# Moving the first experts' weight loads and the normalised-token stores from SP's to ScalarE's transfer queue

## The chip, the cores and the metric

The kernel runs on one core of a Trainium2 chip. The metric is the device time of one execution in microseconds (us); where several executions were timed, their median is given. The names used for the engines are: PE for TensorE (matrix products), DVE for VectorE, ACT for ScalarE, POOL for GpSimd, and SP for SyncE, which in this kernel issues nearly all plain transfers. "Queue" means the line of transfers that one engine issues: SP's, ACT's or POOL's.

## What is computed

The kernel takes 4 × 1024 tokens of width 256, lets them attend to 77 context rows with 16 heads, adds the result, and then runs a mixture of nine experts on the normalised tokens, two experts per token. Cut to what matters:

```python
q = layernorm(x) @ Wq                      # and a scale and shift per head
k, v = split(layernorm(ctx) @ Wkv)
x = x + softmax(q k^T / 8) v @ Wout
xn = (x - mean) / sqrt(var + 1e-5)         # "normalised tokens"
w, idx = top_k(softmax(xn @ Wr), 2)        # two experts per token
hidden = silu(xn @ Wg[e]) * (xn @ Wu[e])   # 256 -> 704
out = x + sum over the two e of w_e * (hidden @ Wd[e])
```

All of it is float32.

## The kernel before

**Two stages.** The tokens are cut into 8 groups (`NG`) of 512, each into 4 sub-blocks (`NS`) of 128. The loop at L1667 runs over the 32 sub-blocks (`i`), with a thirty-third turn that only drains. After it, the loop at L1792 runs over the expert blocks: each takes up to 256 tokens of one expert, gathered through an index list.

**One turn of the attention loop.** PE makes the scores of sub-block `i` in three PSUM banks (`scores`, L295). DVE takes the maxima (L307), ACT the 16 exponentials (`exponentials`, L318), DVE scales them into `an` (L340, L345) and turns them in blocks of 32 (L356) into `anT`. `weights_turn` (L352) sends `anT` to a buffer in device memory, `a_d` (L357); `weights_back` (L360) reads it back in another order with four transfers into `aT` (L366). Both go out from SP. PE uses `aT` of sub-block `i - 3` in `values` (L372), so a sub-block has about three turns for the way out and back. `anT` exists once, so DVE may not turn the next sub-block until `a_d` has landed; `aT` exists three times.

**Once per group.** Counted from the group's last sub-block, the turns are told apart by `sr`. In the turn with `sr == 1` the residual `x` goes to the output (L945) and ACT takes a root. In the turn with `sr == 2` ACT makes the normalised tokens `y` of the group with four activations (`normalised`, L977 to L985). The store of `y` to `y_d` (L988) is put into the list `written` and issued in the same turn after `weights_back` (L1756); for the last two groups it is issued at once (L990). For group 6 that is in the thirty-third turn, for group 7 within the first expert blocks. `y` exists once.

**Weights of an expert block.** `load` (L1360) reads the expert's number from a table into a register (`values_load`), and issues six transfers: the gate weights `Wg` (704 KB), three pieces of the up weights `Wu` (64, 128 and 512 KB) and two of the down weights `Wd` (640 and 64 KB). It is a generator with a stop after `Wg`, after `Wu` and after `Wd`. For the first two blocks (`LEAD = 2`), `first_fetch` (L1658) calls `weights(j, True)`; their generators land in `partly`. The loop takes one step of them per turn (L1752): block 0's `Wg`, `Wu`, `Wd` go out in turns 27, 28 and 29, the one step more that is left ends the generator in turn 30, and all of block 1's go out after the loop (L1766). From block 2 on, `fetch` (L1597) issues a block's weights whole.

**Order of the work.** The order on each engine is that in which the code lists it; nothing is moved by a scheduler. Each engine takes its own list in order, so an instruction that waits holds up those behind it on its engine. The engine that issues a transfer waits for whatever the transfer needs, then goes on once it has issued it.

**The first expert block** (`hidden_pair`, L1437) begins while the last two sub-blocks' `values` are still to be done: after the block's first sixth comes `values(30)`, after the fourth `values(31)` (L1788). For each sixth PE fills one of five PSUM tiles (`mm_tile`), ACT applies Silu (L1450) and DVE multiplies (L1451), which frees the tile. `values` takes a tile of the same five.

Of the kernel before, what the change touches and what calls it, by code (L numbers as in the profile page):

```python
# [15 lines left out]
P = 128  # L16
# [5 lines left out]
def kernel(  # L22
# [18 lines left out]
    nc = tc.nc  # L41
# [6 lines left out]
    E, _, FF = wg.shape  # L48
# [4 lines left out]
    NS = TB // P  # L53
    NG = TOK // TB
    GPB = N // TB
    NF = FF // P
    FT = FF - NF * P
# [55 lines left out]
    y_d = dram.tile([TOK, D], F32, name="y_d")  # L113
# [143 lines left out]
    def off_mean(name, g, mv, r):  # L257

        o = stat.tile([P, NS], F32, tag=name, name=f"{name}{g}")
        nc.vector.scalar_tensor_tensor(o, mv[:, :, 0], -1.0, r, ALU.mult, ALU.mult)  # L260
        return o
# [136 lines left out]
    with ExitStack() as kvs:  # L398
# [23 lines left out]
        for i in range(2):  # L422
            at = slice(i * BH, (i + 1) * BH)
            nc.sync.dma_start(out=cx[:J, at], in_=ctx_in[at].rearrange("b j d -> j b d"))
        wk_v = wkv[:, :INNER].rearrange("(c p) n -> p c n", p=P)
        for i in range(2):
            at = slice(i * INNER // 2, (i + 1) * INNER // 2)
# [226 lines left out]
        def router_weights(pm):  # L654
# [20 lines left out]
            out=before, in_=ones, pattern=[[1, P]], compare_op=ALU.is_gt, fill=0.0, base=0,  # L675
# [48 lines left out]
        for n in range(NP):  # L724
# [7 lines left out]
            for c in range(C):  # L732
                for t in range(2):
# [8 lines left out]
                    at = slice(h * J, (h + 1) * J)  # L742
# [165 lines left out]
    for b in range(B):  # L908
        for m in range(2):
            at = 2 * b + m  # L910
# [66 lines left out]
    def normalised(g):  # L977

        y = pools["rpool"].tile([P, NS, D], F32, tag="y", name=f"y{g}", bufs=1)
        r = routed[g]["r"]  # L980
        o = off_mean("fo", g, routed[g]["mv"], r)
        for s in range(NS):
            yield nc.scalar.activation(
                y[:, s, :], xg[g][:, s, :], AF.Identity,
                bias=o[:, s : s + 1], scale=r[:, s : s + 1],  # L985
            )
        written.append(
            lambda: nc.sync.dma_start(out=y_d.rearrange("(g p s) d -> g p s d", p=P, s=NS)[g], in_=y)  # L988
        )
        if g > NG - 3:  # L990
            written.pop()()
# [108 lines left out]
    tabs = {}  # L1100
# [154 lines left out]
    FA = 4 * P  # L1255
    FB = FF - FA
# [34 lines left out]
    def of(tiles, j):  # L1291

        return tiles[j % len(tiles)]
# [30 lines left out]
    def weights(j, in_parts=False):  # L1324

        _, i, kind = blocks[j]
        if kind == "quad2":
            wgus[j], downs[j] = quads.pop(i)
            return
        if j == LAST:  # L1330
            w, d = late["w", uppers[j][0]], late["d", uppers[j][0]]
        else:
            w = pools["wpool"].tile([P, C, 2 * FF], F32, tag="wgu", name=f"wgu{j}")
            d = of(wds, next_down[0])
            next_down[0] += 1
        more = uppers.get(j, ()) if j < LAST else ()
        wgus[j] = (w, *(late["w", n] for n in more))
        downs[j] = (d, *(late["d", n] for n in more))
        if kind == "quad":
            quads[i] = wgus[j], downs[j]  # L1340
        at = PARTS[kind] * i
        parts = load(tabs[kind][0][0:1, at : at + 1], w, d)
        if in_parts:
            partly.append(parts)
        else:
            advance(parts)

    def weights_upper(k):

        def begin(j):  # L1350
            _, i, kind = blocks[j]
            sets = uppers.get(j, ()) if j < LAST else ()
            if k <= len(sets):
                at = PARTS[kind] * i + len(sets) - k + 1
                n = sets[-k]
                advance(load(tabs[kind][0][0:1, at : at + 1], late["w", n], late["d", n]))

        return begin

    def load(number, w, d):  # L1360
        e = nc.values_load(number, engines=[mybir.EngineType.SP], min_val=0, max_val=E - 1)
        wg_v = wg.rearrange("e (c p) f -> e p c f", p=P)[bass.ds(e, 1)].rearrange("o p c f -> (o p) c f")
        wu_v = wu.rearrange("e (c p) f -> e p c f", p=P)[bass.ds(e, 1)].rearrange("o p c f -> (o p) c f")


        nc.sync.dma_start(out=w[:, :, 0:FF], in_=wg_v)
        yield True
        nc.sync.dma_start(out=w[:, :, FF : FF + FT], in_=wu_v[:, :, NF * P :])
        nc.sync.dma_start(out=w[:, :, FF + FT : FF + FB], in_=wu_v[:, :, FA : NF * P])
        nc.sync.dma_start(out=w[:, :, FF + FB :], in_=wu_v[:, :, 0:FA])  # L1370
        yield True
        nc.sync.dma_start(
            out=d[:, 0:NF, :],
            in_=wd[bass.ds(e, 1), 0 : NF * P, :].rearrange("o (f p) d -> p (o f) d", p=P),
        )
        nc.sync.dma_start(
            out=d[64:128, NF, :], in_=wd[bass.ds(e, 1), NF * P : FF, :].rearrange("o p d -> (o p) d")
        )
        yield True
# [217 lines left out]
    def fetch():  # L1597

        end = known()
        lead_y = LEAD_Y if late else LEAD  # L1600
        for name, fn, lead in (
            ("weights", weights, LEAD), *(UPPER if late else ()),
            ("inputs", inputs, lead_y), ("tokens", tokens, lead_y + 2),
        ):
            if name == "inputs":

                while ahead["tokens"] < min(now[0] + lead_y + 1, end):
                    advance(tokens(ahead["tokens"]))
                    ahead["tokens"] += 1
            while ahead[name] < min(now[0] + lead + 1, end):  # L1610
                got = fn(ahead[name])
                if name in ("inputs", "tokens"):
                    advance(got)
                ahead[name] += 1
# [8 lines left out]
    def advance(what, n=None):  # L1623

        for _ in range(n) if n is not None else iter(int, 1):
            if next(what, None) is None:
                return True
        return False

    def routing(g):  # L1630

        yield from residual(g)
        root(g)
        yield from logits(g)
        exponential(g)
        yield from normalised(g)
        yield from choices(g)
        yield from listed(g)
# [19 lines left out]
    def first_fetch():  # L1658

        for j in range(LEAD):  # L1660
            weights(j, True)
        for fn, j in ((tokens, 0), (tokens, 1), (inputs, 0), (inputs, 1), (tokens, 2), (tokens, 3)):
            first_gathers.append(iter(fn(j)))
        ahead.update(weights=LEAD, inputs=LEAD, tokens=LEAD + 2)

    chosen, early = None, None
    for i in range(N_SUB + 1):  # L1667
        g, s = divmod(i, NS)
        now_on = i < N_SUB
        d = i - LAG  # L1670
# [72 lines left out]
        if gr >= 0 and sr == 2 and q >= 0:  # L1743
            advance(logits(q))
            exponential(q)
            advance(normalised(q))
# [106 lines left out]
```

## Time and profile before

| | us |
|---|---|
| median of 14 runs | 847.28 |
| lowest and highest of them | 846.46, 848.81 |
| the profiled execution, its own time | 848.72 |
| its span, first to last instruction | 847.0 |
| PE busy | 833.2 (98%) |
| DVE busy | 579.5 (68%) |
| ACT busy | 373.5 (44%) |
| POOL busy | 306.6 (36%) |
| transfers, SP's queue | 166.96 MB, 63.2% of the 16 transfer engines' time |
| transfers, ACT's queue | 70 packets |

The profile is of one execution. Times are counted from the first instruction. A timeline line gives the start, the length, the engine (with a "q" for its sequencer, which issues transfers), the source line, the operation, what is written and read, and in brackets the idle time of the engine before it with what ended that. In the table of stretches, each engine has its busy time in a stretch; behind them stand the granted PE clock (1.00 is full), the mean busy share of the 16 transfer engines, and GB/s. PE's ends are modelled, so a PE that is shown busy throughout can still have lost a little.

### The profile page before, as it was taken

The page shows a single profiled execution, that of the slowest core. Times are in us where ns is not written, and L with a number is a line of the kernel's source. Part 1 is how long each engine was busy: PE and PEld are TensorE (multiplying, and loading weights), DVE is VectorE, ACT ScalarE, POOL GpSimd, SP SyncE. Part 2 cuts the span into 40 slices and gives each one's busy share as a digit, 9 for nine tenths or more (in the row PEclk, how much of TensorE's full clock was granted, in tenths as well). Part 3 has the DMA queues.
Part 4 walks back from the last instruction along what each step waited for, and adds up shares of the span by engine and source line. Part 5 has one row for each costly group of instructions (what it writes and reads, how often), then busy time and mean ns, then how long its engine had stood idle before and what let it go on. Part 6 is the DMA issues. An engine that isn't in the chain of part 4 may idle for free. (4 is left out here: it accounts for less than half of the span.)

```text
span 847.0 us, 20860 instructions
## 1 busy us (share of the span) xinstructions
PE 833.2 (98%) x7334; PEld 593.5 (70%) x7334; DVE 579.5 (68%) x1887; ACT 373.5 (44%) x1543; POOL 306.6 (36%) x344
## 2 busy tenths in 40 slices
PE   9999999999999998999999999999999999999996
PEld 6634444556564554788889878788778878877895
DVE  5767779898889976445854585484678566667551
ACT  4778787888868876152222212222222222222221
POOL 3100000123331232577654444544444463453522
PEclk9999999999999999999999999999999999999998
DMA  8028778778678797996885799689779888788511
GB/s 292 7 100 229 201 215 234 220 237 246 190 220 250 219 282 223 311 276 159 212 250 126 204 349 349 178 251 323 203 231 351 262 239 275 214 247 255 117 24 19
DMA packets 129448, 186.04 MB, mean 220 GB/s; under 512 B 26167, under 2 KB 95295, under 8 KB 129216
## 3 DMA queue, kind: packets, MB, share of 16 engines
q1 hardware_dynamic: 111930, 166.96, 63.2%
q0 software_dynamic: 17344, 17.75, 11.8%
q8 instruction: 58, 0.95, 0.5%
q14 instruction: 46, 0.38, 0.1%
q10 hardware_dynamic: 70, 0.00, 0.0%
HBM read 141.08 MB, written 45.00 MB: 220 GB/s over the span
## 5 line engine op out<-in xcount | busy, mean ns | idle before, releaser
L1444 PE MATMUL pg<-xT,wgu 128*128 128x256 f32 x1100 | 243.1, 380 | 0.1
L1444 PEld LDWEIGHTS pg<-xT,wgu 128*128 128x128 f32 x1100 | 208.3, 190 | 30.1 <-issue 1.3
L1560 POOL DMA_INDIRECT out_dram<-co,ids x73 | 116.7, 1598 | 205.8 <-ACT co L1542 133.6
L318 ACT ACTIVATE ex<-psc,mx 128x77 f32<-128x77 f32 x512 | 158.6, 331 | 62.3 <-DVE mx L307 60.1
L1539 PE MATMUL po<-wd,hid 128*128 128x256 f32 (+2 forms) x768 | 173.2, 380 | 0.0
L1539 PEld LDWEIGHTS po<-wd,hid 128*128 128x128 f32 (+2 forms) x768 | 138.7, 183 | 28.6 <-issue 6.2
L143 PE MATMUL po<-u,aT 128*32 128x265 f32 x2560 | 151.6, 390 | 3.9 <-DMA aT<-a_d 3.9
L1417 DVE STREAM_TRANSPOSE xT<-yin 32x128 f32<-32x128 f32 (+1 forms) x528 | 144.7, 274 | 9.0
L1070 POOL DMA_INDIRECT list_d<-line,r_pli x64 | 63.2, 987 | 240.9 <-DVE mx L307 159.8
L1451 DVE TENSOR_TENSOR hid<-pg,sl 128x256 f32<-128x256 f32 x130 | 55.0, 423 | 117.5 <-ACT sl L1450 114.7
L143 PEld LDWEIGHTS po<-u,aT 128*32 128x32 f32 x2560 | 92.1, 110 | 59.4 <-issue 4.7
L1450 ACT ACTIVATE sl<-pg 128x256 f32<-128x256 f32 x130 | 49.7, 383 | 179.7 <-PE pg L1444 171.3
L143 PE MATMUL psc<-g,aT 128*32 128x462 f32 (+1 forms) x1296 | 118.7, 510 | 0.0
L318 ACT ACTIVATION_READ_ACCUMULATOR ex<-psc,mx 128x1 f32 x512 | 108.2, 211 | 0.0
L143 PEld LDWEIGHTS psc<-g,aT 128*32 128x32 f32 x1296 | 46.7, 109 | 60.0 <-issue 47.3
L1542 ACT ACTIVATE co<-po,ids 128x256 f32<-128x256 f32 x66 | 31.1, 474 | 124.2 <-PE po L1539 124.2
L1383 POOL DMA_INDIRECT yin<-y_d,ids x66 | 69.1, 1046 | 35.8 <-issue 22.0
L307 DVE TENSOR_REDUCE mx<-psc 128x6 f32<-128x462 f32 (+1 forms) x96 | 54.1, 564 | 20.6 <-PE psc L143 20.4
L356 DVE STREAM_TRANSPOSE anT<-an 128x1536 f32<-128x1536 f32 x32 | 56.6, 1769 | 6.7 <-DMA a_d<-anT 6.7
L1529 DVE STREAM_TRANSPOSE hid<-hs 32x160 f32<-32x160 f32 (+1 forms) x112 | 39.5, 353 | 1.6
L340 DVE TENSOR_TENSOR an<-ex,rs 128x1024 f32<-128x1024 f32 x32 | 39.2, 1226 | 1.1
L1472 PEld LDWEIGHTS pt<-xT,wgu 128*128 128x128 f32 x308 | 35.1, 192 | 2.1 <-issue 2.0
(378 smaller groups left out, 766.1 us busy)
## 6 DMA issues: line engine op xcount, KB each, us to landing
a_d<-anT SPq DMA_DIRECT2D x32, 768.0 KB
aT<-a_d SPq DMA_DIRECT2D x128, 192.0 KB
wgu<-in_L_ffn_Wg_dram SPq DMA_DIRECT2D x33, 704.0 KB
wd<-in_L_ffn_Wd_dram SPq DMA_DIRECT2D x33, 640.0 KB
wgu<-in_L_ffn_Wu_dram SPq DMA_DIRECT2D x33, 512.0 KB
w_up<-in_L_ffn_Wg_dram SPq DMA_DIRECT2D x12, 704.0 KB
d_up<-in_L_ffn_Wd_dram SPq DMA_DIRECT2D x12, 640.0 KB
w_up<-in_L_ffn_Wu_dram SPq DMA_DIRECT2D x12, 512.0 KB
```

Source lines behind the costliest of these rows:

```text
L143: nc.tensor.matmul(out[a : a + Q], left(a), right, **kw)
L307: return nc.vector.tensor_reduce(nmx[i][:, h : h + n], psc[:, : n * J].rearrange("p (h j) -> p h j", h=n), AX.X, ALU.max, negate=True,)
L318: nc.scalar.activation(exs[i][:, h + q, :], pscs[k][:, q * J : (q + 1) * J], AF.Exp, bias=nmx[i][:, h + q : h + q + 1], accum_out=sms[i][: ...
L356: made = nc.vector.transpose(turned, an_of[0].rearrange("p (k q t) -> p q k t", q=NQ, t=Q))
L1070: i = nc.gpsimd.indirect_dma_start(out=list_d[:, :], out_offset=bass.IndirectOffsetOnAxis(ap=place_i[:, s : s + 1], axis=0), in_=entry.bit ...
L1383: return nc.gpsimd.indirect_dma_start(out=dst, out_offset=None, in_=src, in_offset=bass.IndirectOffsetOnAxis(ap=offsets, axis=0), **kw,)
L1417: yield nc.vector.transpose(xT[q : q + Q].rearrange("p c (h t) -> p h c t", t=P)[:, :nh, :, a : a + Q], of(yins, j)[a : a + Q].rearrange(" ...
L1444: nc.tensor.matmul(pg[:, g, :], w[:, c, at : at + P], xT[:, c, :], start=(c == 0), stop=(c == C - 1),)
L1450: nc.scalar.activation(sl, pg[:, 0, :], AF.Silu)
L1451: made = nc.vector.tensor_tensor(hid[:, f, :], pg[:, 1, :], sl, ALU.mult)
L1539: nc.tensor.matmul(po[rows, :D], hid[:, f, at], d[:, f, :], start=(f == 0), stop=(f == NF))
L1560: i = nc.gpsimd.indirect_dma_start(out=out_r, out_offset=bass.IndirectOffsetOnAxis(ap=ids[j][:, h, word : word + 1], axis=0), in_=cos[j][: ...
```

## The change

The store of `y`, for all eight groups, is issued from ACT's queue, and so are the register load and the six weight transfers of the first two expert blocks. All other transfers stay on SP, the later blocks' weights among them. The places in the code, and so the place of each transfer between the other instructions of its engine, are otherwise as before.

```diff
         written.append(
-            lambda: nc.sync.dma_start(out=y_d.rearrange("(g p s) d -> g p s d", p=P, s=NS)[g], in_=y)
+            lambda: nc.scalar.dma_start(out=y_d.rearrange("(g p s) d -> g p s d", p=P, s=NS)[g], in_=y)
         )
         if g > NG - 3:
             written.pop()()
...
-        parts = load(tabs[kind][0][0:1, at : at + 1], w, d)
+        parts = load(tabs[kind][0][0:1, at : at + 1], w, d, nc.scalar if in_parts else nc.sync)
...
-    def load(number, w, d):
-        e = nc.values_load(number, engines=[mybir.EngineType.SP], min_val=0, max_val=E - 1)
+    def load(number, w, d, queue=nc.sync):
+        e = nc.values_load(number, engines=[queue.engine], min_val=0, max_val=E - 1)
...
-        nc.sync.dma_start(out=w[:, :, 0:FF], in_=wg_v)
+        queue.dma_start(out=w[:, :, 0:FF], in_=wg_v)
         yield True
-        nc.sync.dma_start(out=w[:, :, FF : FF + FT], in_=wu_v[:, :, NF * P :])
-        nc.sync.dma_start(out=w[:, :, FF + FT : FF + FB], in_=wu_v[:, :, FA : NF * P])
-        nc.sync.dma_start(out=w[:, :, FF + FB :], in_=wu_v[:, :, 0:FA])
+        queue.dma_start(out=w[:, :, FF : FF + FT], in_=wu_v[:, :, NF * P :])
+        queue.dma_start(out=w[:, :, FF + FT : FF + FB], in_=wu_v[:, :, FA : NF * P])
+        queue.dma_start(out=w[:, :, FF + FB :], in_=wu_v[:, :, 0:FA])
         yield True
-        nc.sync.dma_start(
+        queue.dma_start(
             out=d[:, 0:NF, :],
             in_=wd[bass.ds(e, 1), 0 : NF * P, :].rearrange("o (f p) d -> p (o f) d", p=P),
         )
-        nc.sync.dma_start(
+        queue.dma_start(
             out=d[64:128, NF, :], in_=wd[bass.ds(e, 1), NF * P : FF, :].rearrange("o p d -> (o p) d")
         )
         yield True
```

## The prediction, made before the change was run

> **What bounds the kernel now.** I first read the busy times: PE is at work 833.2 us of 847.0. Then the waits, sorted by engine: in the whole attention loop PE waits only twice, 3.9 us in all, both times for `aT`. Then the table of stretches, cut at the loop's turns of about 8.7 us, around the place where the first weights go out:
>
> ```profile
> 276.40:285.10 8.70, 8.70 (x148) 4.24 (x144) 8.25 (x29) 5.60 (x34) 2.48 (x5) 1.00 0.65 186
> 285.10:293.80 8.70, 8.70 (x133) 4.18 (x129) 8.36 (x24) 8.18 (x35) 2.02 (x2) 1.00 0.79 243
> 293.80:302.50 8.70, 8.70 (x133) 4.21 (x126) 6.59 (x17) 8.69 (x50) 1.97 (x2) 1.00 1.04 275
> 302.50:311.10 8.60, 8.60 (x132) 5.00 (x132) 6.79 (x24) 4.19 (x27) 2.01 (x2) 1.00 0.90 259
> 311.10:320.10 9.00, 9.00 (x148) 4.95 (x140) 7.87 (x21) 6.02 (x38) 2.53 (x5) 1.00 0.99 298
> 320.10:329.30 9.20, 5.31 (x87) 3.42 (x85) 6.94 (x21) 6.60 (x32) 4.06 (x4) 1.00 0.75 219
> 329.30:338.00 8.70, 8.70 (x97) 4.86 (x101) 3.98 (x11) 5.38 (x10) 1.10 (x1) 0.80 0.82 246
> ```
>
> The columns behind the length are PE, weight loads, DVE, ACT, POOL, then clock, transfer share and GB/s. Before 293.8 PE is full and the transfer engines have a fifth to a third left. From 293.8 to 320.1, while block 0's weights go out, the transfer engines are full (1.04, 0.90, 0.99), and right behind it PE has only 5.31 of 9.20 us, then a clock of 0.80. PE's timeline names it:
>
> ```profile
> 321.68 4.69 PE L143 MATMUL po<-u,aT 128*32 128x265 f32 x80 [1.55 <-DMA aT<-a_d]
> ...
> 329.30 6.37 PE L143 MATMUL po<-u,aT 128*32 128x265 f32 x80 [2.34 <-DMA aT<-a_d]
> ```
>
> The second is also 6.37 - 4.69 = 1.68 us longer at the lower clock. So 1.55 + 2.34 + 1.68 = 5.57 us is all that a better order of transfers can bring in this stage; elsewhere PE has no wait to give back. Last I read SP's own timeline there:
>
> ```profile
> 291.64 0.42 SPq L1366 DMA_DIRECT2D wgu<-in_L_ffn_Wg_dram  x1
> 293.63 1.76 SPq L366 DMA_DIRECT2D aT<-a_d  x4
> 296.10 0.34 SPq L357 DMA_DIRECT2D a_d<-anT  x1
> 296.65 0.41 SPq L1368 DMA_DIRECT2D wgu<-in_L_ffn_Wu_dram  x1
> 297.25 0.91 SPq L1369 DMA_DIRECT2D wgu<-in_L_ffn_Wu_dram  x1
> 299.95 0.37 SPq L1370 DMA_DIRECT2D wgu<-in_L_ffn_Wu_dram  x1
> 304.35 2.26 SPq L366 DMA_DIRECT2D aT<-a_d  x4
> 306.66 0.48 SPq L988 DMA_DIRECT2D y_d<-y  x1
> ```
>
> `aT` (304.35) can only go out when `a_d` (296.10) has landed, 8.25 us later. In a quiet turn that is 5.2 us (279.95 to 285.15). And the third `Wu` is held until 299.95: SP's waits put 1.6 us there on `Wg`, which is the eighth transfer before it. The trace's semaphore numbers show the reason: plain transfers take eight numbers in rotation, and one waits until the transfer eight places earlier has landed. ACT's three small loads at the kernel's start took numbers of the same rotation as SP's.
>
> **Part 1: stores of `y`, groups 0 to 5, on ACT.** SP loses an issue of 0.34 to 0.48 us (one of 1.62) per group; ACT gains it, and must first let its own `y` finish. Queued behind it on ACT are the next turn's 16 exponentials; DVE's scaling waits for these. By the trace, from turn 6 on DVE starts scaling 1.6 us or more (mostly 2.3 to 3.2) after the last exponential, and a bank's maxima begin over 4 us after its earlier exponentials ended, some 1.7 us of which are the scores. Cover is thus 1.6 us or more against about 0.5 us: 0. Without it, 6 x 0.5 = 3 us. Ends: 0 to +3; I take 0, the margin being in the same turns.
>
> **Part 2: block 0's weights on ACT, turns 27 to 29.** ACT takes the register load (SP's first took 1.51 us, with about 0.5 us of register work to the issue), `Wg` 0.4, then `Wu` 0.4 + 0.9 + 0.4, `Wd` 0.9 + 1.4 (SP's rows, partly waiting). ACT has no idle time from 289.05 to 304.8, then waits 1.52 and 2.89 us for DVE; a shift of about 2 us in turns 27 and 28 fits the 1.6 us of DVE's cover and the 1.52 only just. I take 0, ends 0 to +2.
>
> What matters more is the order of the transfers. Now `Wg` is issued at 291.64, while SP waits for `a_d`, and its data fill the transfer engines before `aT`. From ACT it can't go out before the two table loads of that turn end, near 294: 2.3 us of transfer time lie idle in front of the full stretch. Then `Wu`, `y` and `Wd` follow on a queue of their own, beside `a_d` and `aT` instead of before or behind them. The trace has no row for ACT's queue under load. Ends: if SP's transfers pass as if alone, all 5.57 us come back; if ACT's go first, the start lost (2.3 us) and a `Wu` in front of an `aT` (704 KB at 275 GB/s, 2.6 us) make it +4.9. The full share says that the sum of the work decides, and that it starts later; against that, `y` no longer stands between `aT` and `a_d`. I take +0.8: the middle of the ends, -0.3, moved by half of the 2.3 us that start late.
>
> Here the Trainium skill bears ("DMA: Bandwidth & Descriptors", section "Issuing engines are not separate DMA queues"): transfers from all engines run on the same 16 transfer engines and interleave, so a second issuing engine saves only issue time. The shares of 0.90 to 1.04 agree that there is no idle bandwidth to win; by the rule alone the gain of 5.57 us would be close to 0, by the first row (an `a_d` in a quiet turn) it would be all of it. No row here shows the sharing itself.
>
> **Part 3: `y` of group 6 and block 1's weights on ACT, 336.3 on.**
>
> ```profile
> 334.23 2.06 ACT L983 ACTIVATE y<-x,fo,r_r 128x256 f32<-128x256 f32 x4
> 336.30 1.28 ACT L1450 ACT_TABLE_LOAD   x1
> 337.63 0.38 ACT L1450 ACTIVATE sl<-pg 128x256 f32<-128x256 f32 x1
> 344.17 0.38 ACT L1450 ACTIVATE sl<-pg 128x256 f32<-128x256 f32 x1 [6.16 <-PE pg L1444]
> ```
>
> On SP this series took from 340.73 to 346.99, 6.26 us. On ACT it stands before the first Silu, which moves to 337.63 + 6.26 = 343.9. Behind it waits DVE's product, which frees the first of five PSUM tiles; `values(31)` needs that tile at 347.52. With Silu and product 0.8 us, cover is 347.52 - 344.7 = 2.8 us. But `aT` of sub-block 31 is issued by SP from 338.43 to 340.16, in the same rotation of eight, and these take some 6 us to land; seven transfers of ACT among them make the last ones wait until about 345 to 347.5, then table load, Silu and product end 2.1 us later, at 347 to 349.6. The stall is 0 to 2.1 us, and up to 1 us more because `aT(31)` shares with 2.1 MB of weights. Ends 0 to +3; I take +1.0. If the waits are there, the routing work of DVE (12 steps of 0.22 us between products) comes late next. The gain for SP, block 2's weights some 5 us earlier, is worth 0: PE doesn't wait for weights anywhere.
>
> **Part 4: `y` of group 7 on ACT.**
>
> ```profile
> 364.99 1.28 ACT L1450 ACT_TABLE_LOAD   x1
> ...
> 370.59 0.58 ACT L1433 COPY xT<-px 128x512 f32<-128x512 f32 x1
> ```
>
> Here ACT makes `y` until 364.98 and is late: DVE waited 4.27 us for the Silu after the table load, then ran without a gap to the product at 369.68, which releases the Silu at 370.19 and the copy at 370.59. PE's next block starts at 371.23, just as the copy ends at 371.17; it was free at 371.09. The issue, 0.34 us plus the wait for `y`, goes through: +0.4 (0 to +0.5).
>
> **Sum.** 0 + 0 + 0.8 + 1.0 + 0.4 = +2.2 us. The profiled execution took 848.72 (span 847.0), so it would be 850.9; it lies 1.44 over the median of 847.28, which becomes 849.5.
>
> **Rivals.**
> *Faster.* SP's queue holds only `a_d` and `aT` from turn 27 on. Place: the chain a_d, aT, PE of sub-blocks 27 to 29; price: up to -5.57. It decides if `aT(28)` lands by 320.1 instead of 321.7 and `a_d(29)` follows 2.3 us earlier. For it: 8.25 against 5.2 us for an `a_d`. Against: the full transfer share. With part 4: 847.28 - 5.57 + 0.4 = 842.1 in full, half of it 844.9.
> *No change.* The sum of transfers is the same, the waits of the rotation fall into ACT's 6.16 us, and only part 4 shows: 847.7.
> *Much slower.* `y` of group 5 is the eighth behind an `a_d` by the code's order: ACT then waits at 301.3 until `a_d` lands at 304.3, 3.0 + 0.5 us, which exceeds the cover of 1.6 by 1.9 us; with Part 3 at its end (+3) and 0.8 + 0.4: 847.28 + 6.1 = 853.4. Against it: the rotation may follow the time of issue, and then `y` comes before the four `aT` and waits for older ones.
>
> **How the numbers follow.** Forecast (848.98 to 851.5) 0.40, much slower 0.18, no change 0.22, faster 0.20. A measurement of this kernel tells about 0.2%, 1.7 us, from no change. So slower 0.58, same 0.22, faster 0.20. The time is the forecast's, 849.5, its own range 848.0 to 851.5. The range for 8 in 10 goes from 844.9 (half the gain of the faster case) to 853.4 (the much slower one).
>
> **What would show it.** Right: the two waits of PE for `aT` remain at about 4 us or grow; in ACT's timeline the first Silu of block 0 begins at 344 or later, behind issues of L1366 to L1376; `values(31)` starts after 348; the copy at L1433 for block 2 is some 0.4 us later against `y`. Wrong: the waits for `aT` shrink below 2 us with the clock at 1.00 through 338, which is the faster case; or ACT stands still at L988 in turn 28, which is the much slower one.

## The result and the profile after

The changed kernel takes 856.09 us (median; 855.5 to 857.38), the kernel before beside it 847.44: a ratio of 1.0101, with a 95% interval of 1.0091 to 1.011, or 8.65 us more. The forecast of slower came true, its size did not: 849.5 was foretold, 853.4 was the end of the range. The profiled execution has a span of 853.9 us and a time of 855.6, against 847.0 and 848.72. In three of the five sets of experiments the kernel before itself took 870 to 872 us, and not 847 to 848; one chip gave both, why is open, and ratios are compared within a set only.

PE's waits of the changed kernel (what PE waited for, us in all, times, longest):

```profile
PE po L143 <- DVE hid L1451: 5.1, 1, 5.1
PE po L143 <- DMA aT<-a_d: 3.1, 3, 2.4
```

The waits for `aT` went from 3.9 us to 3.1, and one of 5.1 us is new. PE's timeline says where:

```profile
320.91 4.69 PE L143 MATMUL po<-u,aT 128*32 128x265 f32 x80 [0.23 <-DMA aT<-a_d]
328.64 6.37 PE L143 MATMUL po<-u,aT 128*32 128x265 f32 x80 [2.45 <-DMA aT<-a_d]
...
336.86 4.69 PE L143 MATMUL po<-u,aT 128*32 128x265 f32 x80
...
352.06 7.08 PE L143 MATMUL po<-u,aT 128*32 128x265 f32 x80 [5.13 <-DVE hid L1451]
```

These are `values(28)` to `values(31)`. The first three start 0.77, 0.66 and 0.66 us earlier than before (321.68, 329.30, 337.52): up to there the change has gained. `values(31)` starts at 352.06 instead of 347.52, after 5.13 us of standing, and takes 7.08 us instead of 4.69. So 5.13 + 2.39 - 0.66 = 6.86 us, against 6.9 us in the span: the whole difference of these two executions lies in this one step. The medians are 8.65 apart. The profiled execution of the kernel before lay 1.3 us over its median (848.72, 847.44) and that of the changed kernel 0.5 under it (855.6, 856.09); what these 1.8 us are, the pair of profiles doesn't show.

The profile names DVE's product `hid` (L1451) as what ended the wait. The timelines of ACT, DVE and SP say otherwise:

```profile
335.65 0.34 ACTq L988 DMA_DIRECT2D y_d<-y  x1
336.80 0.39 ACTq L1366 DMA_DIRECT2D wgu<-in_L_ffn_Wg_dram  x1
337.37 0.60 ACTq L1368 DMA_DIRECT2D wgu<-in_L_ffn_Wu_dram  x1
...
339.24 0.38 ACTq L1372 DMA_DIRECT2D wd<-in_L_ffn_Wd_dram  x1
342.97 0.52 ACTq L1376 DMA_DIRECT2D wd<-in_L_ffn_Wd_dram  x1
343.51 1.28 ACT L1450 ACT_TABLE_LOAD   x1 [7.89 <-DMA wgu<-in_L_ffn_Wu_dram]
344.81 0.66 ACT L1450 ACTIVATE sl<-pg 128x256 f32<-128x256 f32 x2
```

```profile
345.22 0.42 DVE L1451 TENSOR_TENSOR hid<-pg,sl 128x256 f32<-128x256 f32 x1 [9.65 <-ACT sl L1450]
...
351.18 0.75 DVE L1451 TENSOR_TENSOR hid<-pg,sl 128x256 f32<-128x256 f32 x2
```

```profile
332.77 0.34 SPq L357 DMA_DIRECT2D a_d<-anT  x1
339.69 4.53 SPq L366 DMA_DIRECT2D aT<-a_d  x4
```

The first Silu starts at 344.81, and its product, which frees the tile for `values(31)`, ends at 345.64, before PE was free at 346.93. Two later products end by 351.93, close to PE's start, but they free other tiles: in `e8_act_late2` below, `values(31)` starts before any of the later products. `aT(31)` is what was late: its four transfers took SP from 339.69 to 344.22 to issue (before: 1.73 us from 338.43), and their last increment, by the trace's semaphore events, came at 351.86 instead of 344.54. PE starts 0.2 us behind it. The stretches, columns as before, show what the transfer engines did then:

```profile
338.00:347.50 9.50, 8.93 (x88) 6.29 (x80) 2.00 (x10) 2.32 (x4) 0.00 (x0) 1.00 1.01 278
347.50:352.00 4.50, 0.00 (x0) 0.00 (x0) 4.18 (x23) 0.38 (x1) 2.04 (x2) 0.79 1.06 319
352.00:360.00 8.00, 7.94 (x84) 4.44 (x85) 1.05 (x4) 0.00 (x0) 5.96 (x9) 0.69 0.77 224
```

They are full (1.01, 1.06) while PE has nothing (0.00 of 4.50 us), and then PE runs at a granted clock of 0.69. In the kernel before, block 1's weights were issued from 343.18 on, behind `aT(31)`; now they are issued from 336.80 on, before it. Their 2112 KB need 7.8 us at the 278 GB/s of that stretch; `aT(31)` came 7.3 us later.

### The profile page after: what moved, and what is told of

Read it like the earlier page. It is cut to its first block, busy times and chain, and to the rows that moved or that the text cites. A ratio compares the mean times of both kernels' runs of the same rounds, so it can differ in the third digit from the quotient of the medians.

```text
span 853.9 us, 20863 instructions
## 1 busy us (share of the span) xinstructions
PE 835.5 (98%) x7334; PEld 593.6 (70%) x7334; DVE 578.5 (68%) x1887; ACT 373.2 (44%) x1543; POOL 306.6 (36%) x344
## 5 line engine op out<-in xcount | busy, mean ns | idle before, releaser
L143 PE MATMUL po<-u,aT 128*32 128x265 f32 x2560 | 153.9, 394 | 8.2 <-DVE hid L1451 5.1
L1451 DVE TENSOR_TENSOR hid<-pg,sl 128x256 f32<-128x256 f32 x130 | 54.9, 423 | 123.3 <-ACT sl L1450 121.9
```

The lines of the kernel that those rows point to most:

```text
L143: nc.tensor.matmul(out[a : a + Q], left(a), right, **kw)
L1451: made = nc.vector.tensor_tensor(hid[:, f, :], pg[:, 1, :], sl, ALU.mult)
```

## Experiments

**Which part?** Four kernels put one part alone, or two, on ACT's queue, in one set:

```diff
 e1_y:   y of all groups
+lambda: nc.scalar.dma_start(out=y_d...[g], in_=y)
 e2_w0:  block 0's weights alone;  e3_w1:  block 1's alone (j == 1)
+parts = load(..., nc.scalar if in_parts and j == 0 else nc.sync)
 e4_y_w0: y and block 0's weights
```

> Only the stores of y go out from ACT; all weights stay on SP. If the loss lies with block 1's weights (theory A), this kernel keeps the time of before within 1.5 us, and PE starts the last product of the attention (values of sub-block 31) at 347 to 348 us as before. If the loss is spread over the transfers that were moved (theory B: each group's store costs about 1 us on ACT), it is some 4 to 8 us slower.

> Only block 0's weights (turns 27 to 29) go out from ACT. Theory A: within 1.5 us of before. Theory B, and the step of the prediction that put 0.8 us there: 1 to 3 us slower, with PE's waits for aT of sub-blocks 28 and 29 longer than 1.55 and 2.34 us.

> Only block 1's weights go out from ACT, after the loop. Theory A: the whole loss is here, 7 to 9 us slower than before; PE waits about 5 us before the values of sub-block 31, and these then take about 7 us at a lowered clock. Theory B: 2 to 3 us slower.

> The change without block 1: y and block 0's weights from ACT, block 1's from SP. Theory A: the time of before or up to 1 us less, since the waits for aT of sub-blocks 28 and 29 were 0.8 us shorter in the changed kernel. Theory B: about two thirds of the loss, 5 to 6 us slower.

Beside 847.12 us: `e1_y` 847.02 (0.9998; 0.9989 to 1.0006), `e2_w0` 848.73 (1.0019; 1.0007 to 1.003), `e4_y_w0` 848.07 (1.0014; 1.0 to 1.0027), and `e3_w1` 853.31 (1.0083; 1.0065 to 1.0101). Block 1's weights alone bring most of the loss; without them on ACT the rest costs about 1 us. PE's timeline of `e3_w1`:

```profile
335.43 4.69 PE L143 MATMUL po<-u,aT 128*32 128x265 f32 x80 [1.08 <-DMA aT<-a_d]
349.05 6.37 PE L143 MATMUL po<-u,aT 128*32 128x265 f32 x80 [3.55 <-DMA aT<-a_d]
```

`values(31)` waits for `aT` here by the profile's own words, and runs at the lowered clock.

**Is it the late ACT?** The forecast's stall went through the Silu, the product and a PSUM tile. `e5_act_late` and, again in another set, `e8_act_late2` are the kernel before with 19 small copies on ACT in front of the first Silu, and no transfer moved.

```diff
+for _ in range(19):
+    nc.scalar.activation(hids[1][0:64, NF, :], hids[1][0:64, NF, :], AF.Copy)
```

> The kernel before, with 19 more small copies of zeros on ACT (about 7 us) in front of the first Silu of block 0, at the place where the change puts block 1's transfers. ACT comes as late as in the changed kernel (first Silu near 344.8), but the transfers are as before. Theory A1 (PE waits for aT of sub-block 31, which shares the transfer engines with the weights): time of before within 1 us, the values of sub-block 31 start at 347 to 348. Theory A2 (PE waits for a PSUM tile that DVE's product frees, late because Silu is late): about 7 us slower, a wait of about 5 us.

> Again the kernel before with ACT kept at work for about 7 us in front of the first Silu of block 0, since the first run of it fell on a chip on which every kernel takes 2 to 3% longer. Theory A1 (PE waits for aT of sub-block 31): within 1 us of before, no wait before the values of sub-block 31. Theory A2 (a PSUM tile): about 7 us slower.

`e5_act_late` took 868.1 us beside 870.34 (0.9977; 0.9956 to 0.9997), `e8_act_late2` 848.08 beside 847.92 (1.0007; 0.9996 to 1.0018). In `e8_act_late2` ACT begins the Silu later than in the changed kernel, and PE doesn't wait:

```profile
336.50 8.47 ACT L1769 ACTIVATE hid<-hid 64x256 f32<-64x256 f32 x19
344.98 1.28 ACT L1450 ACT_TABLE_LOAD   x1
346.27 0.66 ACT L1450 ACTIVATE sl<-pg 128x256 f32<-128x256 f32 x2
```

```profile
346.69 0.42 DVE L1451 TENSOR_TENSOR hid<-pg,sl 128x256 f32<-128x256 f32 x1 [10.03 <-ACT sl L1450]
...
350.36 0.41 DVE L1451 TENSOR_TENSOR hid<-pg,sl 128x256 f32<-128x256 f32 x1
```

```profile
337.95 4.69 PE L143 MATMUL po<-u,aT 128*32 128x265 f32 x80
347.95 4.69 PE L143 MATMUL po<-u,aT 128*32 128x265 f32 x80
```

`values(31)` starts at 347.95, behind the first product (over at 347.11) and ahead of the second (350.36), so it needs the first alone. A late ACT of this size costs nothing.

**Is it the order alone?** `e6_sp_first` and, again, `e9_sp_first2` leave everything on SP and only issue block 1's weights before `aT(31)`.

```diff
+if i == N_SUB:
+    for parts in partly:
+        advance(parts)
```

> The kernel before, with block 1's weights issued from SP just before the four transfers of aT of sub-block 31 instead of after them; ACT issues nothing. Theory A1: aT comes behind 2.1 MB of weights, some 6 us later; PE waits 3 to 6 us before the values of sub-block 31, 5 to 8 us slower in all. Theory A2: ACT is on time, so the time of before within 1 us.

> Again the kernel before with block 1's weights in front of aT of sub-block 31 on SP's own queue. Theory A1: PE waits 2.5 us or more before the values of sub-block 31, which then run at a lowered clock; 4 to 8 us slower. If A1 holds only for a second queue: within 1 us of before.

`e6_sp_first` took 868.8 beside 870.34 (1.0006; 0.9984 to 1.0029), though `values(31)` waited 2.6 us there; `e9_sp_first2` took 851.95 beside 847.92 (1.004; 1.0018 to 1.0062). In its SP and PE timelines the weights are out at 334.58 to 338.80, `aT(31)` follows at 339.61, and `values(31)` starts at 350.10:

```profile
334.58 0.41 SPq L1366 DMA_DIRECT2D wgu<-in_L_ffn_Wg_dram  x1
...
338.30 0.50 SPq L1376 DMA_DIRECT2D wd<-in_L_ffn_Wd_dram  x1
339.61 2.18 SPq L366 DMA_DIRECT2D aT<-a_d  x4
```

```profile
350.10 6.37 PE L143 MATMUL po<-u,aT 128*32 128x265 f32 x80 [2.08 <-DMA aT<-a_d]
```

The order alone, without a second queue, makes a loss of 3.4 us by the ratio, 4.0 by the medians.

**And behind it?** `e7_act_behind` is the changed kernel with block 1's weights, still on ACT, issued behind the Silu of the block's fourth sixth.

```diff
-for parts in partly:
-    advance(parts)
...
+in_first[3].append(lambda: [advance(parts) for parts in partly])
```

> The changed kernel, with block 1's weights still from ACT, but behind the Silu of the fourth sixth of block 0, when aT of sub-block 31 has nearly landed. Both theories: the wait before the values of sub-block 31 is gone. What is left is whether the weights come in time for block 1: they go out near 348 instead of 337 and are needed near 355, so PE may wait up to 5 us there. Between before and 5 us slower; if the queue of ACT were slow by itself, as slow as the changed kernel.

It took 871.12 beside 870.34 (1.0017; 0.9993 to 1.004). PE came to `values(31)` without a wait, at 351.45, 10.0 us after `values(30)` as before; in its place PE waited for block 1's `xT`, 13.4 us in three waits. The gain of the better order can't be read from this set.

**The rotation, or the sharing?** In the changed kernel and in `e3_w1` SP didn't issue `aT(31)` when `a_d(31)` had landed (338.25 and 337.18), but at 339.69 and 340.86: by the semaphore numbers, `y` of group 6 in the one and `Wg` in the other held the number that SP's transfer needed, until they had landed (339.62 and 340.79). In the changed kernel the third of the four waited for the first `Wu` in the same way (issued 343.19, `Wu` landed 343.17). POOL's transfers don't take numbers of this rotation. So `e10_pool`, and `e16_pool2` in another set, issue block 1's weights from POOL's queue:

```diff
-parts = load(...)
+parts = load(..., nc.gpsimd if in_parts and j == 1 else nc.sync)
```

> Block 1's weights alone (all six pieces) go out from POOL's queue instead of SP's; everything else as before. They leave at about the time they left ScalarE's queue in e3_w1 (some 332 to 338 us), so they share the transfer engines with a_d(31) and aT(31) as there, but POOL's transfers don't take numbers of the rotation of eight that SP's and ScalarE's share. Theory R (the rotation: SP holds aT(31)'s issue until Wg's number is free, 337.18 to 340.81 in e3_w1): aT(31) is issued as soon as a_d(31) lands, and about half of e3's loss or more goes: +0 to +3.5 us (below 1.004). Theory S (order and sharing alone: 2.1 MB in front of or beside 0.4 MB): aT(31) is issued at once but its packets still end about 348, values(31) starts near 349 at the lowered clock, +5 to +7 us (1.006 to 1.0085) as e3.

> As e10_pool. Theory S after e10_pool (a_d(31) took 10.9 us to land beside block 1's weights, with no number of the rotation shared): 1.007 to 1.011 on this chip too, with a_d(31) landing over 9 us after its issue. Theory R: below 1.004, with aT(31) issued within 0.5 us of a_d(31)'s landing some 5 us after its issue.

> e3_w1 once more, for comparison on this chip: both theories 1.0083 (1.0065 to 1.0101), 6 to 7 us; on a chip where PE waits for xT, less.

`e10_pool` took 878.63 beside 870.78 (1.0095; 1.0061 to 1.0129), `e16_pool2` 880.52 beside 871.9 (1.0106; 1.0071 to 1.014); `e11_e3_again`, with the rotation, 872.0 beside 870.78 (1.0008; 0.9984 to 1.0031). `values(31)` waits 2.53 us in it as well; why so little of this reaches the end, in a trace where PE also waits 6.4 us for `xT`, is open. The timelines of POOL, SP and PE in `e16_pool2`:

```profile
330.03 0.81 POOL L1366 DMA_DIRECT2D wgu<-in_L_ffn_Wg_dram  x1 [0.38 <-issue]
...
333.84 0.63 POOL L1376 DMA_DIRECT2D wd<-in_L_ffn_Wd_dram  x1
```

```profile
337.83 0.34 SPq L357 DMA_DIRECT2D a_d<-anT  x1
349.24 1.73 SPq L366 DMA_DIRECT2D aT<-a_d  x4
```

```profile
347.47 6.12 PE L143 MATMUL po<-u,aT 128*32 128x265 f32 x80 [6.49 <-DMA aT<-a_d]
```

The wait of 6.49 us is that of `values(30)`, for `aT(30)`. Behind it `a_d(31)`, 768 KB, takes 11.4 us from issue to `aT(31)`, where the kernel before needs 5.2 (333.24 to 338.43). Sharing the transfer engines is enough for a loss of this size; no number was held. But it is not the same collision: POOL issues the weights 6.8 us earlier than ACT did (330.03 against 336.80), and they meet `aT(30)` and `a_d(31)`. What the rotation adds for itself in the changed kernel wasn't isolated.

**Which pieces?** In `e13_small_sp` three large pieces of block 1's weights go from ACT, and the three small ones from SP, behind `aT(31)`.

```diff
 queue.dma_start(out=w[:, :, 0:FF], in_=wg_v)
-queue.dma_start(out=w[:, :, FF : FF + FT], ...)
-queue.dma_start(out=w[:, :, FF + FT : FF + FB], ...)
+rest.dma_start(out=w[:, :, FF : FF + FT], ...)
+rest.dma_start(out=w[:, :, FF + FT : FF + FB], ...)
 queue.dma_start(out=w[:, :, FF + FB :], ...)
...
-queue.dma_start(out=d[64:128, NF, :], ...)
+rest.dma_start(out=d[64:128, NF, :], ...)
```

> As e3_w1, but of block 1's six pieces only the three large ones (Wg, the 512-column Wu, the large Wd) go from ScalarE's queue; the three small ones follow aT(31) on SP's. The numbers of the rotation then fall otherwise: aT(31)'s transfers meet numbers of earlier aT's and are issued when a_d(31) lands, and the large Wu waits on ScalarE's queue for aT(31)'s third transfer. Only Wg (0.72 MB) can be in front of aT(31). Theory R and theory S both expect less than e3_w1's loss: R +0 to +2 us, S +1 to +3 us (Wg's 0.72 MB at about 300 GB/s are 2.4 us, against a slack of 1 us).

It took 879.97 beside 870.78 (1.0069; 1.0036 to 1.0103): more than either theory, R or S, expected. Its timelines of ACT, DVE and PE:

```profile
340.04 0.44 ACTq L1368 DMA_DIRECT2D wgu<-in_L_ffn_Wg_dram  x1
348.72 0.41 ACTq L1372 DMA_DIRECT2D wgu<-in_L_ffn_Wu_dram  x1
350.60 0.38 ACTq L1374 DMA_DIRECT2D wd<-in_L_ffn_Wd_dram  x1
351.01 1.28 ACT L1452 ACT_TABLE_LOAD   x1 [12.43 <-DMA out_dram<-x]
352.31 0.66 ACT L1452 ACTIVATE sl<-pg 128x256 f32<-128x256 f32 x2
```

```profile
352.72 0.42 DVE L1453 TENSOR_TENSOR hid<-pg,sl 128x256 f32<-128x256 f32 x1 [15.52 <-ACT sl L1452]
```

```profile
353.20 6.59 PE L143 MATMUL po<-u,aT 128*32 128x265 f32 x80 [2.98 <-DVE hid L1453]
```

Here the forecast's mechanism does act: the large `Wu` waits on ACT for the third transfer of `aT(31)` (landed 348.70, issued 348.72) and the large `Wd` for the store of the residual (landed 350.58, issued 350.60), ACT gets to its Silu at 352.31, the product ends at 353.14, and PE starts at 353.20, though `aT(31)` had landed at 349.29. The wait that the profile names is genuine in this kernel and was not in the changed one; the ends of the first product (353.14 here, 345.64 there) and of `aT(31)` (349.29 and 351.86) tell the two apart.

**What does `y` in front add?** `e12_y67_sp`, and `e15_y67_sp2` beside `e14_after_again` (the changed kernel), put `y` of the last two groups back on SP. `y` of group 7 comes after `values(31)`, so what differs there is `y` of group 6.

```diff
-lambda: nc.scalar.dma_start(out=y_d...[g], in_=y)
+lambda: (nc.sync if g > NG - 3 else nc.scalar).dma_start(out=y_d...[g], in_=y)
```

> The changed kernel with the normalised tokens of its last two groups back on SP's queue; groups 0 to 5 and both blocks' weights stay on ScalarE's. If the changed kernel's last 2.4 us over e3_w1 come from y of group 6 in front of block 1's weights (its number held aT(31)'s first transfer until 339.62, ScalarE's issues behind it were later, and aT(31)'s last transfers met Wu's numbers), this one is +6 to +7 us (1.007 to 1.0085). If they come from block 0's weights or the earlier groups, it stays at +8.5 to +9 (1.010).

> The changed kernel once more, to stand beside the next two on the same chip: 1.0101 (1.0091 to 1.011) where the kernel before takes about 847 us; on a chip where it takes about 870, PE also waits for xT and part of the loss is covered: 1.002 to 1.006.

> As e12_y67_sp, on a chip shared with the changed kernel. If y of group 6 in front of block 1's weights makes the last 2.4 us, this is some 2 us below e14_after_again and aT(31) lands about 2.5 us earlier against values(30); if not, the two are equal within 0.1%.

`e12_y67_sp` took 873.64 beside 870.78 (1.0023; 0.9998 to 1.0049). In the other set, beside 871.9, `e14_after_again` took 880.98 (1.0098; 1.0063 to 1.0132) and `e15_y67_sp2` 873.47 (1.002; 0.9995 to 1.0044): 7.5 us apart, more than the 2 us expected. ACT and PE in `e14_after_again`:

```profile
341.54 0.34 ACTq L988 DMA_DIRECT2D y_d<-y  x1
342.69 0.39 ACTq L1366 DMA_DIRECT2D wgu<-in_L_ffn_Wg_dram  x1
```

```profile
356.74 7.58 PE L143 MATMUL po<-u,aT 128*32 128x265 f32 x80 [6.77 <-DVE hid L1451]
```

and in `e15_y67_sp2`:

```profile
337.76 0.40 ACTq L1366 DMA_DIRECT2D wgu<-in_L_ffn_Wg_dram  x1
```

```profile
352.42 7.37 PE L143 MATMUL po<-u,aT 128*32 128x265 f32 x80 [1.88 <-DMA aT<-a_d]
```

With `y` in front, block 1's weights start 4.9 us later (342.69 against 337.76) and end later; `values(31)` starts 4.3 us later. (The 7.37 us in `e15_y67_sp2` are at the full granted clock, 1.00; PE's weight loads pause there for some 0.6 us at a time, for no cause that the profile shows.) The changed kernel stands to `e3_w1` in the same way: `Wg` issued at 336.80 against 333.60, `aT(31)` landed at 351.86 against 348.95. There the times (856.09 and 853.31, from different sets) differ by less, and the intervals of the ratios touch, so the share of `y` in the 8.65 us is not settled.

**A version that is a little faster than both.** `c1_down_last` leaves all on SP and puts block 0's `Wd`, which no block of the attention loop needs, off until after the loop, behind block 1's weights; `c2_y_down_last` adds all `y` on ACT.

```diff
-elif partly and i < N_SUB - 1 and advance(partly[0], 1):
+elif partly and i < N_SUB - 3 and advance(partly[0], 1):
...
-for parts in partly:
+for parts in reversed(partly):
```

> The kernel before, all on SP, with block 0's down weights put off from turn 29 until after the loop, behind block 1's weights. If PE's waits for aT of sub-blocks 28 and 29 come from the weights' share of the transfer engines, aT of 28 lands some 2 us earlier: 2 to 4 us faster than before. If they come from the way out and back itself: no change. The down weights are needed near 365 and should land near 356.

> The same, and the stores of y from ACT's queue. If the stores are free on ACT and no longer stand between aT and the next a_d: as fast as the version with the down weights put off, or up to 1 us faster.

Beside 847.92 us: 847.15 (0.9989; 0.9975 to 1.0003) and 845.98 (0.9986; 0.9977 to 0.9995). The first, expected 2 to 4 us faster, can't be told from no change. The second is faster by 1.2 us (0.4 to 2.0, from the interval); in its profile PE's waits for `aT` are 2.9 us, and `values(29)` keeps the full clock:

```profile
327.10 4.69 PE L143 MATMUL po<-u,aT 128*32 128x265 f32 x80 [1.84 <-DMA aT<-a_d]
```

It keeps it in the profile of `e1_y` too, after 2.09 us, and `e1_y` is no faster than the kernel before; so what makes the 1.2 us is not shown.

## Why the prediction was wrong in size

**Part 1, `y` of groups 0 to 5 at 0: right.** `e1_y`, with all eight, is at 0.9998.

**Part 2, block 0's weights at +0.8: inside its error, its reasons half wrong.** `e2_w0` measures +1.6 us (0.6 to 2.5, from the interval), `e4_y_w0` +1.0. But in the profile of the changed kernel this stage gains 0.66 us. The 2.3 us of late start weren't there either: ACT issued `Wg` at 290.88, beside a table load (290.60 to 291.88) and not behind two of them near 294; SP had issued it at 291.64. The two rivals of this stage fall with it. The faster one wanted the waits for `aT` below 2 us; they are 3.1, with the clock at 0.80 from 329.3 to 338.0 as before. The much slower one wanted ACT to stand at L988 until 304.3; `y` of group 5 went out at 300.86.

**Part 3, block 1's weights at +1.0: this is the step that failed.** It had two terms. "The stall is 0 to 2.1 us", by Silu, product and PSUM tile, was 0: the first Silu came at 344.81, as foretold ("344 or later"), but the tile was free before PE. "Up to 1 us more because `aT(31)` shares with 2.1 MB of weights" was the term that decided, and it measured 5.13 us of waiting and 2.39 us of lowered clock. The numbers for it could be had beforehand: 2112 KB at the 275 GB/s used in Part 2 are 7.9 us. In the trace of the kernel before, `aT(31)` landed 3.0 us before `values(31)` began (344.54 and 347.52), so weights wholly in front of it would cost an estimated 7.9 - 3.0 = 4.9 us, and the lowered clock 1.68 more, as it did at `values(29)`: +6.6. The forecast had done this sum for one `Wu` in Part 2 and not for six transfers here. It took for granted that `aT(31)`, issued at about the same time, would be served among the weights at little cost; in fact the weights were issued before it, and SP's wait for `a_d(31)`, which used to hold them back, no longer did so. Two of the forecast's signs came true all the same, the first Silu behind 344 and `values(31)` behind 348; that is luck, since the one did not cause the other.

The rotation was foretold in one direction, ACT's weights waiting for `aT(31)`'s numbers. Among these runs that is seen in `e13_small_sp`; in the changed kernel ACT's last `Wd` waited for ACT's own `Wg` (landed 342.95, issued 342.97). There it worked in the other direction, SP's `aT(31)` waiting for numbers that ACT's `y` and `Wu` held. What that cost wasn't isolated, but `aT(31)` is what PE needs next.

The Trainium skill states in "DMA: Bandwidth & Descriptors" ("Issuing engines are not separate DMA queues") that transfers from all engines interleave on the same 16 transfer engines. The shares of 1.01 and 1.06, and 11.4 us for an `a_d` beside weights from POOL's queue, agree; and one conclusion from it was missed in the forecast: if the queues share the engines, a queue's waits are an order, and moving a bulk load away from them takes this order away.

**Part 4, `y` of group 7 at +0.4: it was 0.** ACT's timeline of the changed kernel:

```profile
371.92 1.28 ACT L1450 ACT_TABLE_LOAD   x1
371.93 0.35 ACTq L988 DMA_DIRECT2D y_d<-y  x1
```

The issue ran beside the table load, not in front of it. The copy that was to come 0.4 us later against `y` starts 5.6 us behind it in both kernels (364.98 and 370.59 before, 371.91 and 377.47 now), and `e1_y` has no loss to show.

## What to carry to other kernels

A queue does more than issue: the waits in it keep what stands behind them from the transfer engines. Before moving a bulk load to another queue, look at what SP was waiting for in front of it, and price the move as the load's bytes over the measured rate, less the slack of the transfer that it can now overtake. This is an estimate: for the same 2112 KB in front, 7.8 us by the rate, `aT(31)` landed 8.0 us later than before in the changed kernel, 6.5 in `e3_w1` and 5.0 in `e9_sp_first2`, each counted from the start of `values(30)`. Where the profile names one releaser of a wait on several things, compare the time of each with the moment when the engine moved on.

## What the runs showed of the hardware

- **A transfer issued behind bulk landed late, whichever queue the bulk was on.** `aT(31)` took 4.8 us from its last issue to its last increment before (339.73 to 344.54), 8.3 with the weights on ACT's queue (343.53 to 351.86) and 8.8 with them in front on SP's own (341.18 to 350.02 in `e9_sp_first2`); `a_d(31)` took 11.4 us with them on POOL's, against 5.2.
- **In this program one rotation of eight semaphore numbers serves SP and ACT.** SP stood up to 3.6 us (337.18 to 340.79) for a transfer that ACT had issued.
- **ACT issues a transfer while it loads a table** (371.92 and 371.93; 290.60 and 290.88).
- **The clock after a wait isn't a function of the wait alone.** 2.30 us (`values(29)` in `e3_w1`) was followed by 4.69 us of work, but 2.34 (before) and 2.08 (`values(31)` in `e9_sp_first2`) by 6.37, and 5.13 by 7.08. The Trainium skill ("TensorE: Matmul & The Clock Gate", "What's actually happening") describes a free-running window of activity of some 3.4 us. The traces agree: in each of the 20, while the kernel works, the granted clock changes only at points that lie whole multiples of 3.41 us apart. Stretches between such points, the kernel before first, then `e9_sp_first2`, then `e3_w1`:

```profile
326.87:330.28 3.41, 1.07 (x21) 0.61 (x24) 2.97 (x9) 3.35 (x8) 2.75 (x3) 1.00 1.04 331
330.28:333.70 3.42, 3.42 (x38) 1.62 (x34) 2.42 (x5) 0.56 (x2) 0.39 (x1) 0.50 0.58 166
...
346.80:350.22 3.42, 1.34 (x10) 0.89 (x12) 1.66 (x7) 0.38 (x1) 2.54 (x3) 1.00 1.06 346
350.22:353.63 3.41, 3.41 (x36) 2.04 (x37) 0.00 (x0) 0.00 (x0) 2.51 (x6) 0.50 1.08 327
...
325.86:329.28 3.42, 1.55 (x28) 0.94 (x32) 2.65 (x7) 3.36 (x6) 2.81 (x3) 1.00 1.02 346
329.28:332.69 3.41, 3.41 (x58) 1.88 (x51) 3.02 (x8) 0.46 (x3) 0.04 (x1) 1.00 0.56 142
```

With PE busy for 1.07 or 1.34 us of a stretch, the next one ran at 0.50; with 1.55 us, at 1.00. Near 1.5 us the traces show both (1.50 in the changed kernel from 350.15, then 0.50; 1.44 in `e11_e3_again` from 349.26, then 1.00). The 2.30 us in `e3_w1` lay across such a point, 0.43 us of them before it. So a wait of 2.08 us, shorter than the window, was enough where it fell into one.
